# A pre-activation convolution on one core: contrasts in one small matmul, fewer columns, packed bias, fillers, and whole-image transfers

## The chip, the cores and the metric

The kernel runs on one core of a Trainium2 chip. The metric is the device time of one execution in microseconds. Three runs of the kernel before gave 89.01, 90.0 and 90.27 us; the median is 90.0.

## The reference

For each of 8 images with 32 channels of 128 x 128 the input is normalized over 16 groups (2 channels each), convolved with a 3 x 3 kernel of 32 output channels, given a bias, and added to the input. The convolution is written with Fourier transforms on 256 x 256, and what is cut out of it starts at (256 - 128) / 2:

```python
sh = (fft_H - out_h) // 2          # 64
out = sp[:, :, sh:sh + out_h, sw:sw + out_w]
return out + bias[None, :, None, None]
...
m = jnp.mean(g, axis=(2, 3, 4), keepdims=True)   # per group of 2 channels
s = jnp.var(g, axis=(2, 3, 4), keepdims=True)
return ((g - m) / jnp.sqrt(s + eps)).reshape(v.shape)
...
x = x + _L0_conv_ref(_gn(x), weight, bias, 1, 1)
```

So output pixel (0, 0) takes what an ordinary full convolution has at (64, 64). The lower right part of the image, 66 x 66 pixels with a border, is all that the convolution reads, and its result is non-zero only in the upper left 66 x 66 of the output. Everywhere else the output is the input plus the bias.

## The kernel before

**Layout.** The host splits every image into its four pixel parities. A core sees each image as a tile `x` of 128 partitions (2 row parities x 2 column parities x 32 channels) by 64 x 64 pixels, 2 MB in f32. All 8 images stay in SBUF. A 3 x 3 convolution becomes 2 x 2 taps of full 128 x 128 matrices in this layout. N is 33: a convolution reads pixels 31 to 63 in both directions, and writes rows and columns 0 to 32.

**Transfers.** SP issues every transfer but one, in program order: the first image in four pieces, the weights `w_sb`, then each image in two halves (line 68); later the stores of line 176. The bias, 128 rows of 4 bytes, is issued by ACT (line 71). SP's transfers take eight semaphores in turn, so each transfer waits on SP until the one eight issues earlier has landed. Transfers of one queue are worked off in the order of issue.

**Statistics.** For each image DVE runs eight `bn_stats` (line 109) and an aggregate (`mv`, line 116). PE multiplies the means with `avg`, which averages over the eight partitions of a group (`ps_m`, line 120); DVE takes three small steps (lines 125 to 128); PE averages the deviations and variances (`ps_v`, line 134). ACT takes the root (line 140), DVE the reciprocal and the product with the mean (lines 142, 143), and ACT writes the normalized pixels to `g` (line 147), a 34 x 34 tile whose last row and column are zeros; there are two of them, used in turn. ACT then adds the bias to the parts of the image that the convolution does not touch (lines 153 and 155).

**Convolution.** `multiply` covers 11 of the 33 rows in four matmuls of 363 columns, one for each tap (line 162); in f32 each shows as two records in the trace. `add` (line 171) adds the bias and the image to the sum, in place in `x`. A loop over the images writes the order out by hand: it puts the small matmuls of the next image between the chunks of the present one, and the statistics of the image after that between the `add`s. The lower half of an image (rows 33 to 63) is stored as soon as its bias is added, the upper part after its third `add`.

Of the kernel before, what the change touches and what calls it, by code (L numbers as in the profile page):

```python
# [24 lines left out]
F32 = mybir.dt.float32  # L25
AF = mybir.ActivationFunctionType
ALU = mybir.AluOpType

P = 128
EPS = 1e-5  # L30
FFT = 256
STATS = 8


@with_exitstack
def conv_preact_kernel(
    ctx: ExitStack,
    tc: tile.TileContext,
    x: bass.AP,
    weight: bass.AP,  # L40
    bias: bass.AP,
    out: bass.AP,
):
    nc = tc.nc

    B, _, H, W = x.shape
    C = P // 4
    LO = (FFT - 2 * H) // 4 - 1
    N = H - LO
    ROWS = 11  # L50
    NCHUNK = N // ROWS
    NSTAT = H // STATS

    cpool = ctx.enter_context(tc.tile_pool(name="const", bufs=1))
    xpool = ctx.enter_context(tc.tile_pool(name="x", bufs=1))
    spool = ctx.enter_context(tc.tile_pool(name="small", bufs=2))
    ps_conv = ctx.enter_context(tc.tile_pool(name="ps_conv", bufs=6, space=bass.MemoryType.PSUM))
    ps_stat = ctx.enter_context(tc.tile_pool(name="ps_stat", bufs=1, space=bass.MemoryType.PSUM))


    xts = [xpool.tile([P, H, W], F32, name=f"x{img}") for img in range(B)]
    w_sb = cpool.tile([P, 4, P], F32, name="w_sb")
    bias_sb = cpool.tile([P, 1], F32, name="bias_sb")
    for img in range(B):
        parts = 4 if img == 0 else 2
        for k in range(parts):
            rows = slice(k * H // parts, (k + 1) * H // parts)
            nc.sync.dma_start(xts[img][:, rows, :], x[img, :, rows, :])  # L68
        if img == 0:
            nc.sync.dma_start(w_sb, weight)  # L70
            nc.scalar.dma_start(bias_sb, bias)


    pair = cpool.tile([P, P // 2, 2], F32, name="pair")
    nc.gpsimd.memset(pair, 0.125)
    nc.gpsimd.affine_select(  # L76
        out=pair, in_=pair, pattern=[[-2, P // 2], [0, 2]], base=0,
        channel_multiplier=1, compare_op=ALU.is_ge, fill=0.0,
    )
    nc.gpsimd.affine_select(  # L80
        out=pair, in_=pair, pattern=[[2, P // 2], [0, 2]], base=1,
        channel_multiplier=-1, compare_op=ALU.is_ge, fill=0.0,
    )
    pair2 = pair.rearrange("p a b -> p (a b)")
    avg = cpool.tile([P, P], F32, name="avg")
    nc.vector.tensor_add(avg[:, 0 : 2 * C], pair2[:, 0 : 2 * C], pair2[:, 2 * C : 4 * C])  # L86
    nc.vector.tensor_add(avg[:, 2 * C : 3 * C], avg[:, 0:C], avg[:, C : 2 * C])
    for k in (0, 1, 3):
        nc.vector.tensor_copy(avg[:, k * C : (k + 1) * C], avg[:, 2 * C : 3 * C])
    eps = cpool.tile([P, 1], F32, name="eps")  # L90
    nc.vector.memset(eps, EPS * FFT * FFT)

    warm = cpool.tile([P, 1], F32, name="warm")
    nc.scalar.activation(warm, eps, AF.Sqrt)  # L94


    gs = []
    for k in range(2):
        g = cpool.tile([P, N + 1, N + 1], F32, name=f"g{k}")
        nc.gpsimd.memset(g[:, N : N + 1, :], 0.0)  # L100
        nc.gpsimd.memset(g[:, 0:N, N : N + 1], 0.0)
        gs.append(g)

    stats = [cpool.tile([P, NSTAT, 6], F32, name=f"stats{img}") for img in range(B)]
    mvs, ps_ms, ps_vs, means = {}, {}, {}, {}

    def take_stats(img, first, last):
        for s in range(first, last):
            nc.vector.bn_stats(  # L109
                stats[img][:, s, :],  # L110
                xts[img][:, STATS * s : STATS * (s + 1), :].rearrange("p h w -> p (h w)"),
            )

    def aggregate(img):
        mvs[img] = spool.tile([P, 2], F32, tag="mv", bufs=3, name=f"mv{img}")
        nc.vector.bn_aggr(mvs[img], stats[img].rearrange("p n s -> p (n s)"))  # L116

    def group_mean(img):
        ps_ms[img] = ps_stat.tile([P, 1], F32, tag="ps_m", name=f"ps_m{img}")
        nc.tensor.matmul(ps_ms[img], avg, mvs[img][:, 0:1], start=True, stop=True)  # L120

    def deviations(img):

        means[img] = spool.tile([P, 2], F32, tag="mean", name=f"mean{img}")
        nc.vector.tensor_copy(means[img][:, 0:1], ps_ms[img])  # L125
        diff = means[img][:, 1:2]
        nc.vector.tensor_sub(diff, mvs[img][:, 0:1], means[img][:, 0:1])  # L127
        nc.vector.scalar_tensor_tensor(  # L128
            diff, in0=diff, scalar=diff, in1=mvs[img][:, 1:2], op0=ALU.mult, op1=ALU.add
        )  # L130

    def group_variance(img):
        ps_vs[img] = ps_stat.tile([P, 1], F32, tag="ps_v", name=f"ps_v{img}")
        nc.tensor.matmul(ps_vs[img], avg, means[img][:, 1:2], start=True, stop=True)  # L134

    def normalize(img):
        xt, g = xts[img], gs[img % 2]

        std = spool.tile([P, 1], F32, tag="std", name=f"std{img}")
        nc.scalar.activation(std, ps_vs[img], AF.Sqrt, bias=eps, scale=float(FFT * FFT))  # L140
        rstd = spool.tile([P, 2], F32, tag="rstd", name=f"rstd{img}")
        nc.vector.reciprocal(rstd[:, 0:1], std)  # L142
        nc.vector.scalar_tensor_tensor(  # L143
            rstd[:, 1:2], in0=means[img][:, 0:1], scalar=-1.0, in1=rstd[:, 0:1],
            op0=ALU.mult, op1=ALU.mult,
        )
        nc.scalar.activation(  # L147
            g[:, 0:N, 0:N], xt[:, LO:H, LO:W], AF.Identity,
            bias=rstd[:, 1:2], scale=rstd[:, 0:1],
        )  # L150

        low = xt[:, N:H, :].rearrange("p h w -> p (h w)")
        nc.scalar.activation(low, low, AF.Identity, bias=bias_sb)  # L153
        right = xt[:, 0:N, N:W]
        nc.scalar.activation(right, right, AF.Identity, bias=bias_sb)  # L155

    def multiply(img, n):
        g = gs[img % 2]
        ps = ps_conv.tile([P, ROWS, N], F32, tag="ps", name=f"ps{img}_{n}")
        for k in range(4):  # L160
            top, left = n * ROWS + k // 2, k % 2
            nc.tensor.matmul(  # L162
                ps, w_sb[:, k, :], g[:, top : top + ROWS, left : left + N],
                start=(k == 0), stop=(k == 3),
            )
        return ps

    def add(img, n, ps):

        part = xts[img][:, n * ROWS : (n + 1) * ROWS, 0:N]  # L170
        nc.vector.scalar_tensor_tensor(  # L171
            part, in0=ps, scalar=bias_sb, in1=part, op0=ALU.add, op1=ALU.add
        )

    def store(img, first, last):
        nc.sync.dma_start(out[img, :, first:last, :], xts[img][:, first:last, :])

    take_stats(0, 0, NSTAT)
    aggregate(0)
    group_mean(0)  # L180
    deviations(0)
    group_variance(0)
    normalize(0)
    store(0, N, H)
    take_stats(1, 0, NSTAT)
    aggregate(1)
    for img in range(B):
        more, yet_more = img + 1 < B, img + 2 < B
        ps = multiply(img, 0)
        if more:  # L190
            group_mean(img + 1)
            deviations(img + 1)
        add(img, 0, ps)
        if yet_more:
            take_stats(img + 2, 0, NSTAT // 2)
        ps = multiply(img, 1)
        if more:
            group_variance(img + 1)
            normalize(img + 1)
            store(img + 1, N, H)  # L200
        add(img, 1, ps)
        if yet_more:
            take_stats(img + 2, NSTAT // 2, NSTAT)
            aggregate(img + 2)
        ps = multiply(img, 2)
        add(img, 2, ps)
        store(img, 0, N)


# [36 lines left out]
```

## Time and profile before

| | before |
|---|---|
| median of three runs | 90.0 us |
| the profiled execution | 90.13 us |
| its span | 88.2 us |
| PE busy | 67.2 us (76%) |
| DVE busy | 60.6 us (69%) |
| ACT busy | 37.9 us (43%) |
| moved by DMA | 33.84 MB, 384 GB/s over the span |

Busy times are summed over the span; the span is the time from the first to the last event of one profiled execution, and the execution's own time has 1.93 us beside it. The page divides the span into 40 slices of 2.2 us; a digit is a busy share in tenths. A window row gives a stretch's start and end, its length, the granted PE clock, the share in which the 16 DMA engines were busy (it can pass 1 in short stretches, since packets are counted where they start), and GB/s. A row of the chain or of the timeline gives start, length, engine, line and what ran.

### The profile page before, as it was taken

Reading aid. Unit: us, or ns where it says so; the run is one execution under the profiler, and the core shown is the slowest. Engines: PE = TensorE matmul, PEld = TensorE weight load, DVE = VectorE, ACT = ScalarE, POOL = GpSimd, SP = SyncE. Lnnn points to the kernel's source line nnn. Section 1 sums busy time; section 2 is a strip of 40 time slices with the busy share of each in tenths; the row PEclk is TensorE's granted clock in tenths of the full one; section 3 lists DMA queues with packets and bytes.
Section 4 is the critical chain, followed back from the end, with each engine's and each line's share of the span. In section 5 each row is a group of like instructions: output and inputs, shape, how many; then the busy total and the mean of one; then the engine's idle time right before and its main releaser. Section 6 shows DMA issues by size and latency. Waiting matters only on the chain.

```text
span 88.2 us, 744 instructions
## 1 busy us (share of the span) xinstructions
PE 67.2 (76%) x224; PEld 41.5 (47%) x224; DVE 60.6 (69%) x142; ACT 37.9 (43%) x34; POOL 2.1 (2%) x11
## 2 busy tenths in 40 slices
PE   0000022599999999999999999999999999999300
PEld 0000022356665665666566556656664666666000
DVE  0308965992999799979979997998899723222200
ACT  4200003970049517922980594189139707910000
POOL 6200000000000000000000000000000000000000
PEclk9999999999999999999999999999999999999997
DMA  1679999999999999999999999999999999799392
GB/s 20 160 283 420 441 416 416 424 416 416 416 424 428 428 420 413 424 416 424 405 415 436 428 422 420 422 439 428 423 427 419 437 431 426 306 401 424 153 391 100
DMA packets 5186, 33.84 MB, mean 384 GB/s; under 512 B 704, under 2 KB 704, under 8 KB 2368
## 3 DMA queue, kind: packets, MB, share of 16 engines
q1 hardware_dynamic: 5040, 33.82, 93.1%
q10 hardware_dynamic: 144, 0.00, 0.1%
q8 instruction: 1, 0.02, 0.1%
q14 instruction: 1, 0.01, 0.0%
HBM read 17.04 MB, written 16.78 MB: 384 GB/s over the span
## 4 chain that ended last, share of the span: by engine, by line
PE 76%; DMA 8%; DVE 7%; ACT 2%; issue 1%; SPq 0%; DVEq 0%
PE ps L162 73%; DMA x<-x_dram 8%; DVE stats L109 4%; PE ps_m L120 2%; PE ps_v L134 2%; ACT g L147 1%; DVE x L171 1%; DVE mv L116 0%; SPq L68 0%; ACT std L140 0%; DVE mean L128 0%; DVE rstd L142 0%; DVE rstd L143 0%; DVE mean L127 0%; DVE mean L125 0%
## 5 line engine op out<-in xcount | busy, mean ns | idle before, releaser
L162 PE MATMUL ps<-g,w_sb 128*128 128x363 f32 x192 | 65.9, 493 | 2.1 <-ACT g L147 2.1
L162 PEld LDWEIGHTS ps<-g,w_sb 128*128 128x128 f32 x192 | 36.1, 197 | 23.5 <-ACT g L147 5.2
L109 DVE BATCH_NORM_STATS2 stats<-x 128x6 f32<-128x512 f32 x64 | 39.5, 679 | 3.4 <-DMA x<-x_dram 3.4
L171 DVE SCALAR_TENSOR_TENSOR x<-ps,bias_sb,x 128x363 f32<-128x363 f32 x24 | 13.8, 576 | 7.0 <-PE ps L162 7.0
L153 ACT ACTIVATE x<-x,bias_sb 128x1984 f32<-128x1984 f32 x8 | 15.6, 1949 | 0.3
L140 ACT ACTIVATE std<-ps_v,eps 128x1 f32<-128x1 f32 x8 | 2.1, 261 | 31.4 <-PE ps_v L134 31.4
L147 ACT ACTIVATE g<-x,rstd 128x1089 f32<-128x1089 f32 x8 | 10.4, 1305 | 5.8 <-DVE rstd L143 4.9
L120 PE MATMUL ps_m<-mv,avg 128*128 128x1 f32 x16 | 2.7, 236 | 12.4 <-DVE mv L116 12.4
L120 PEld LDWEIGHTS ps_m<-mv,avg 128*128 128x128 f32 x16 | 3.4, 222 | 14.4 <-DVE mv L116 12.4
L155 ACT ACTIVATE x<-x,bias_sb 128x1023 f32<-128x1023 f32 x8 | 9.1, 1132 | 0.0
L125 DVE COPY mean<-ps_m 128x1 f32<-128x1 f32 x8 | 1.3, 158 | 5.5 <-PE ps_m L120 5.5
L134 PEld LDWEIGHTS ps_v<-mean,avg 128*128 128x128 f32 x16 | 3.1, 204 | 2.4 <-DVE mean L128 0.8
L116 DVE BATCH_NORM_AGGREGATE mv<-stats 128x2 f32<-128x48 f32 x8 | 3.0, 372 | 0.3
L142 DVE RECIPROCAL rstd<-std 128x1 f32<-128x1 f32 x8 | 1.2, 150 | 2.8 <-ACT std L140 2.8
L134 PE MATMUL ps_v<-mean,avg 128*128 128x1 f32 x16 | 2.5, 227 | 0.7 <-DVE mean L128 0.7
L86 DVE TENSOR_TENSOR avg<-pair 128x64 f32<-128x64 f32 x1 | 0.2, 226 | 2.6 <-POOL pair L80 2.6
L128 DVE SCALAR_TENSOR_TENSOR mean<-mean,mv 128x1 f32<-128x1 f32 x8 | 1.8, 220 | 0.3
L94 ACT ACT_TABLE_LOAD x1 | 1.3, 1283 | 1.2 <-PEq L234 1.2
L127 DVE TENSOR_TENSOR mean<-mv,mean 128x1 f32<-128x1 f32 x8 | 1.3, 159 | 0.3
L143 DVE SCALAR_TENSOR_TENSOR rstd<-mean,rstd 128x1 f32<-128x1 f32 x8 | 1.3, 160 | 0.3
L76 POOL TENSOR_SCALAR_AFFINE_SELECT pair<-pair 128x128 f32<-128x128 f32 x1 | 0.7, 706 | 0.1
L80 POOL TENSOR_SCALAR_AFFINE_SELECT pair<-pair 128x128 f32<-128x128 f32 x1 | 0.7, 706 | 0.1
(11 smaller groups left out, 1.9 us busy)
## 6 DMA issues: line engine op xcount, KB each, us to landing
x<-x_dram SPq DMA_DIRECT2D x14, 1024.0 KB, 19.0
out_dram<-x SPq DMA_DIRECT2D x8, 1056.0 KB, 14.2
out_dram<-x SPq DMA_DIRECT2D x8, 992.0 KB, 15.2
x<-x_dram SPq DMA_DIRECT2D x4, 512.0 KB, 7.3
w_sb<-weight_dram SPq DMA_DIRECT2D x1, 256.0 KB, 8.6
bias_sb<-bias_dram ACTq DMA_DIRECT2D x1, 0.5 KB, 6.0
```

The costliest lines, as they stand in the source:

```text
L94: nc.scalar.activation(warm, eps, AF.Sqrt)
L109: nc.vector.bn_stats(stats[img][:, s, :], xts[img][:, STATS * s : STATS * (s + 1), :].rearrange("p h w -> p (h w)"),)
L116: nc.vector.bn_aggr(mvs[img], stats[img].rearrange("p n s -> p (n s)"))
L120: nc.tensor.matmul(ps_ms[img], avg, mvs[img][:, 0:1], start=True, stop=True)
L128: nc.vector.scalar_tensor_tensor(diff, in0=diff, scalar=diff, in1=mvs[img][:, 1:2], op0=ALU.mult, op1=ALU.add)
L134: nc.tensor.matmul(ps_vs[img], avg, means[img][:, 1:2], start=True, stop=True)
L140: nc.scalar.activation(std, ps_vs[img], AF.Sqrt, bias=eps, scale=float(FFT * FFT))
L147: nc.scalar.activation(g[:, 0:N, 0:N], xt[:, LO:H, LO:W], AF.Identity, bias=rstd[:, 1:2], scale=rstd[:, 0:1],)
L153: nc.scalar.activation(low, low, AF.Identity, bias=bias_sb)
L155: nc.scalar.activation(right, right, AF.Identity, bias=bias_sb)
L162: nc.tensor.matmul(ps, w_sb[:, k, :], g[:, top : top + ROWS, left : left + N], start=(k == 0), stop=(k == 3),)
L171: nc.vector.scalar_tensor_tensor(part, in0=ps, scalar=bias_sb, in1=part, op0=ALU.add, op1=ALU.add)
```

## The change

- **Transfers.** The first image is loaded in pieces of 8, 16, 16, 16 and 8 rows, the second in pieces of 32, 16 and 16, all others whole. Images 0 to 5 are stored whole after the last `add`; images 6 and 7 in parts. The bias and a small matrix `signs` lie behind the weights in one tile `wb_sb`, which SP loads; ACT issues no transfer.
- **Statistics.** ACT multiplies `signs` by each partition's mean and scales the variance (`terms`, 9 columns). One small matmul with `avg` gives minus the group mean, seven contrasts of the eight means of a group, and the mean variance. ACT squares the contrasts and sums them; with the mean variance this is the group variance. DVE copies one column and takes the reciprocal.
- **Convolution.** `g` is 33 x 33 and has no zeros; taps that would read them leave that row or column out. `g` is written in two parts, the first 12 rows first.
- **Fillers.** Five matmuls with 512 columns on pieces of the first image stand ahead of its small matmul, three behind it. Their results are not read.
- **Order.** The third `add` of an image stands behind the next image's aggregate; two chunks are multiplied before the small matmul, one after.

```diff
-    w_sb = cpool.tile([P, 4, P], F32, name="w_sb")
-    bias_sb = cpool.tile([P, 1], F32, name="bias_sb")
+    wb_sb = cpool.tile([P, 4 * P + 1 + NSIGN], F32, name="wb_sb")
+    bias_sb = wb_sb[:, 4 * P : 4 * P + 1]
+    signs = wb_sb[:, 4 * P + 1 :]
     for img in range(B):
-        parts = 4 if img == 0 else 2
-        for k in range(parts):
-            rows = slice(k * H // parts, (k + 1) * H // parts)
+        pieces = {0: (1, 2, 2, 2, 1), 1: (4, 2, 2)}.get(img, (8,))
+        first = 0
+        for piece in pieces:
+            rows = slice(first, first + piece * STATS)
             nc.sync.dma_start(xts[img][:, rows, :], x[img, :, rows, :])
+            first += piece * STATS
         if img == 0:
-            nc.sync.dma_start(w_sb, weight)
-            nc.scalar.dma_start(bias_sb, bias)
+            nc.sync.dma_start(wb_sb, wb)
...
+        terms = spool.tile([P, NSIGN + 1], F32, tag="terms", name=f"terms{img}")
+        nc.scalar.activation(terms[:, 0:NSIGN], signs, AF.Identity, scale=mv[:, 0:1])
+        nc.scalar.activation(
+            terms[:, NSIGN:], mv[:, 1:2], AF.Identity, bias=eps, scale=float(FFT * FFT)
         )
...
+        nc.tensor.matmul(ps_ms[img], avg, mvs[img], start=True, stop=True)
...
+        nc.scalar.activation(square, contrasts, AF.Square, accum_out=var[:, 0:1])
+        nc.vector.tensor_copy(var[:, 1:2], ps_m[:, NSIGN:])
...
+        nc.scalar.activation(std, var[:, 0:1], AF.Sqrt, bias=var[:, 1:2])
...
+        nc.scalar.activation(rstd[:, 1:2], ps_m[:, 0:1], AF.Identity, scale=rstd[:, 0:1])
+        for rows in (slice(0, ROWS + 1), slice(ROWS + 1, N)):
...
+            dr, dc = k // 2, k % 2
+            rows = min(ROWS, N - dr - n * ROWS)
+            top = n * ROWS + dr
             nc.tensor.matmul(
-                ps, w_sb[:, k, :], g[:, top : top + ROWS, left : left + N],
+                ps[:, 0:rows, 0 : N - dc], wb_sb[:, k * P : (k + 1) * P],
+                g[:, top : top + rows, dc:N],
...
+    for first, times in ((0, 1), (1, 1), (3, 1), (5, 1), (7, 1)):
+        keep_warm(first * STATS, times)
     take_stats(0, 0, NSTAT)
     aggregate(0)
-    group_mean(0)
-    deviations(0)
-    group_variance(0)
+    group(0)
+    keep_warm(0, 3)
     normalize(0)
-    store(0, N, H)
+    add_bias(0)
     take_stats(1, 0, NSTAT)
-    aggregate(1)
     for img in range(B):
-        more, yet_more = img + 1 < B, img + 2 < B
-        ps = multiply(img, 0)
+        more = img + 1 < B
+        ps = [multiply(img, 0), multiply(img, 1)]
         if more:
-            group_mean(img + 1)
-            deviations(img + 1)
-        add(img, 0, ps)
-        if yet_more:
-            take_stats(img + 2, 0, NSTAT // 2)
-        ps = multiply(img, 1)
+            aggregate(img + 1)
+        if img:
+            add(img - 1, 2, last)
+            if img - 1 < B - 2:
+                store(img - 1, 0, H)
+            else:
+                for k in range(B - 2, B):
+                    store(k, N, H)
+                store(img - 1, 0, N)
+        add(img, 0, ps[0])
         if more:
-            group_variance(img + 1)
+            group(img + 1)
             normalize(img + 1)
...
+            add_bias(img + 1)
+        add(img, 1, ps[1])
+        last = multiply(img, 2)
+        if img + 2 < B:
+            take_stats(img + 2, 0, NSTAT)
+    store(B - 1, 0, 2 * ROWS)
+    add(B - 1, 2, last)
+    store(B - 1, 2 * ROWS, N)
```

What now stands where, in rows of the order of each engine (line, operation, written tile <- read tiles, shape; `x_72` to `x_79` are the eight images).

ACT at the program's start, of the kernel before and then of the change:

```order
L71 DMA bias_sb<-bias_dram 128x1
L94 ACT_TABLE_LOAD
L94 ACTIVATE warm<-eps 128x1
L140 ACTIVATE std_148<-ps_v_146,eps 128x1
L147 ACTIVATE g_116<-x_72,rstd_150 128x33x33
L153 ACTIVATE x_72<-x_72,bias_sb 128x1984
```

```order
L96 ACT_TABLE_LOAD
L96 ACTIVATE warm<-eps 128x1
L114 ACTIVATE terms_136<-wb_sb,mv_134 128x8
L115 ACTIVATE terms_136<-mv_134,eps 128x1
L131 ACTIVATE square_144,var_145<-ps_m_139 128x7
L135 ACTIVATE std_148<-var_145 128x1
L138 ACTIVATE rstd_150<-ps_m_139,rstd_150 128x1
L140 ACTIVATE g_110<-x_72,rstd_150 128x396
```

The bias transfer is gone from ACT's queue, and five small operations stand in an image's chain ahead of `g` where one stood.

SP behind its loads, from the first store on, of the kernel before and then of the change:

```order
L176 DMA out_dram<-x_72 128x1984
L176 DMA out_dram<-x_73 128x1984
L176 DMA out_dram<-x_72 128x2112
L176 DMA out_dram<-x_74 128x1984
L176 DMA out_dram<-x_73 128x2112
L176 DMA out_dram<-x_75 128x1984
```

```order
L176 DMA out_dram<-x_72 128x4096
L176 DMA out_dram<-x_73 128x4096
L176 DMA out_dram<-x_74 128x4096
L176 DMA out_dram<-x_75 128x4096
L176 DMA out_dram<-x_76 128x4096
L176 DMA out_dram<-x_77 128x4096
L176 DMA out_dram<-x_78 128x1984
L176 DMA out_dram<-x_79 128x1984
L176 DMA out_dram<-x_78 128x2112
L176 DMA out_dram<-x_79 128x1408
L176 DMA out_dram<-x_79 128x704
```

The lower half of an image no longer goes ahead of the image before it; it waits for the upper part.

DVE for one image in the loop, of the kernel before (from the first `add` of image 1) and then of the change (from the third `add` of image 0):

```order
L171 SCALAR_TENSOR_TENSOR x_73<-ps_0_213,bias_sb,x_73 128x11x33
L109 BN_STATS stats_125<-x_75 128x6 x4
L142 RECIPROCAL rstd_238<-std_236 128x1
L143 SCALAR_TENSOR_TENSOR rstd_238<-mean_220,rstd_238 128x1
L171 SCALAR_TENSOR_TENSOR x_73<-ps_1_229,bias_sb,x_73 128x11x33
L109 BN_STATS stats_125<-x_75 128x6 x4
L116 BN_AGGR mv_250<-stats_125 128x2
L171 SCALAR_TENSOR_TENSOR x_73<-ps_2_252,bias_sb,x_73 128x11x33
```

```order
L171 SCALAR_TENSOR_TENSOR x_72<-ps_2_197,wb_sb,x_72 128x11x33
L171 SCALAR_TENSOR_TENSOR x_73<-ps_0_210,wb_sb,x_73 128x11x33
L132 COPY var_231<-ps_m_228 128x1
L137 RECIPROCAL rstd_236<-std_234 128x1
L171 SCALAR_TENSOR_TENSOR x_73<-ps_1_215,wb_sb,x_73 128x11x33
L104 BN_STATS stats_115<-x_75 128x6 x8
L112 BN_AGGR mv_267<-stats_115 128x2
```

The eight `bn_stats` now stand in one piece behind the reciprocal, with the aggregate behind them, and no other work of DVE lies between.

More of the change, by code (lines that the diff above doesn't have):

```diff
@@ L39, in conv_preact_kernel @@
     x: bass.AP,
-    weight: bass.AP,
-    bias: bass.AP,
+    wb: bass.AP,
     out: bass.AP,
@@ L83, in conv_preact_kernel @@
     )
+    eps = cpool.tile([P, 1], F32, name="eps")
+    nc.vector.memset(eps, EPS * FFT * FFT)
     pair2 = pair.rearrange("p a b -> p (a b)")
@@ L89, in conv_preact_kernel @@
         nc.vector.tensor_copy(avg[:, k * C : (k + 1) * C], avg[:, 2 * C : 3 * C])
-    eps = cpool.tile([P, 1], F32, name="eps")
-    nc.vector.memset(eps, EPS * FFT * FFT)
     warm = cpool.tile([P, 1], F32, name="warm")
     nc.scalar.activation(warm, eps, AF.Sqrt)
[L97 to L102, printed above, removed]
+    gs = [cpool.tile([P, N, N], F32, name=f"g{k}") for k in range(2)]
     stats = [cpool.tile([P, NSTAT, 6], F32, name=f"stats{img}") for img in range(B)]
-    mvs, ps_ms, ps_vs, means = {}, {}, {}, {}
+    mvs, ps_ms = {}, {}
     def take_stats(img, first, last):
@@ L114, in aggregate @@
     def aggregate(img):
[L115 to L129, printed above, removed]
-        )
@@ L132, in group_variance @@
-    def group_variance(img):
-        ps_vs[img] = ps_stat.tile([P, 1], F32, tag="ps_v", name=f"ps_v{img}")
-        nc.tensor.matmul(ps_vs[img], avg, means[img][:, 1:2], start=True, stop=True)
+        mv = spool.tile([P, 2], F32, tag="mv", name=f"mv{img}")
+        nc.vector.bn_aggr(mv, stats[img].rearrange("p n s -> p (n s)"))
+        terms = spool.tile([P, NSIGN + 1], F32, tag="terms", name=f"terms{img}")
+        nc.scalar.activation(terms[:, 0:NSIGN], signs, AF.Identity, scale=mv[:, 0:1])
@@ L139, in normalize @@
         std = spool.tile([P, 1], F32, tag="std", name=f"std{img}")
-        nc.scalar.activation(std, ps_vs[img], AF.Sqrt, bias=eps, scale=float(FFT * FFT))
+        nc.scalar.activation(std, var[:, 0:1], AF.Sqrt, bias=var[:, 1:2])
         rstd = spool.tile([P, 2], F32, tag="rstd", name=f"rstd{img}")
         nc.vector.reciprocal(rstd[:, 0:1], std)
[L143 to L150, printed above, removed]
+        nc.scalar.activation(rstd[:, 1:2], ps_m[:, 0:1], AF.Identity, scale=rstd[:, 0:1])
+        for rows in (slice(0, ROWS + 1), slice(ROWS + 1, N)):
+            nc.scalar.activation(
+                g[:, rows, :], xt[:, LO + rows.start : LO + rows.stop, LO:W], AF.Identity,
+                bias=rstd[:, 1:2], scale=rstd[:, 0:1],
+            )
@@ L160, in multiply @@
         for k in range(4):
-            top, left = n * ROWS + k // 2, k % 2
+            dr, dc = k // 2, k % 2
+            rows = min(ROWS, N - dr - n * ROWS)
+            top = n * ROWS + dr
             nc.tensor.matmul(
-                ps, w_sb[:, k, :], g[:, top : top + ROWS, left : left + N],
+                ps[:, 0:rows, 0 : N - dc], wb_sb[:, k * P : (k + 1) * P],
+                g[:, top : top + rows, dc:N],
                 start=(k == 0), stop=(k == 3),
@@ L176, in store, with keep_warm @@
         nc.sync.dma_start(out[img, :, first:last, :], xts[img][:, first:last, :])
+    ps_w = ps_stat.tile([P, 512], F32, tag="ps_w", name="ps_w")
+    def keep_warm(first, times):
+        piece = xts[0][:, first : first + STATS, :].rearrange("p h w -> p (h w)")
+        for _ in range(times):
+            nc.tensor.matmul(ps_w, avg, piece, start=True, stop=True)
+    for first, times in ((0, 1), (1, 1), (3, 1), (5, 1), (7, 1)):
+        keep_warm(first * STATS, times)
     take_stats(0, 0, NSTAT)
     aggregate(0)
-    group_mean(0)
-    deviations(0)
-    group_variance(0)
+    group(0)
+    keep_warm(0, 3)
     normalize(0)
-    store(0, N, H)
+    add_bias(0)
     take_stats(1, 0, NSTAT)
-    aggregate(1)
     for img in range(B):
-        more, yet_more = img + 1 < B, img + 2 < B
-        ps = multiply(img, 0)
+        more = img + 1 < B
+        ps = [multiply(img, 0), multiply(img, 1)]
         if more:
-            group_mean(img + 1)
-            deviations(img + 1)
-        add(img, 0, ps)
-        if yet_more:
-            take_stats(img + 2, 0, NSTAT // 2)
-        ps = multiply(img, 1)
+            aggregate(img + 1)
[8 more added lines that the diff above has]
+        add(img, 0, ps[0])
         if more:
-            group_variance(img + 1)
+            group(img + 1)
             normalize(img + 1)
[L200 to L207, printed above, removed]
+            add_bias(img + 1)
[6 more added lines that the diff above has]
+    store(B - 1, 2 * ROWS, N)
 def kernel(x, L0_conv_weight, L0_conv_bias):
@@ L225 @@
                 blocks[rin, cin, :, dr, dc, rout, cout, :] = weight[:, :, a, b].T
+    bits = [(-1.0) ** (np.arange(4 * C) // k % 2) for k in (2 * C, C, 1)]
+    signs = -np.ones((4 * C, NSIGN), x.dtype)
+    for k in range(1, NSIGN):
+        signs[:, k] = FFT * np.prod([b for j, b in enumerate(bits) if k >> j & 1], axis=0)
     arrays = {
@@ L230 @@
         ).reshape(B, 4 * C, H // 2, W // 2),
-        "weight_dram": blocks.reshape(4 * C, 4, 4 * C),
-        "bias_dram": np.tile(np.asarray(L0_conv_bias).reshape(C, 1), (4, 1)),
+        "wb_dram": np.concatenate(
+            [
+                blocks.reshape(4 * C, 16 * C),
+                np.tile(np.asarray(L0_conv_bias).reshape(C, 1), (4, 1)),
+                signs,
+            ],
+            axis=1,
+        ),
     }
```

11 lines of the change are left out of this document (10 added, 1 removed).

## The prediction

> **What bounds the kernel now.** The first view is the page's chain of the work that ended last, and beside it the slices and the DMA queue.
>
> ```profile
> span 88.2 us, 744 instructions
> PE 76%; DMA 8%; DVE 7%; ACT 2%; issue 1%; SPq 0%; DVEq 0%
> DMA  1679999999999999999999999999999999799392
> GB/s 20 160 283 420 441 416 416 424 416 416 416 424 428 428 420 413 424 416 424 405 415 436 428 422 420 422 439 428 423 427 419 437 431 426 306 401 424 153 391 100
> q1 hardware_dynamic: 5040, 33.82, 93.1%
> ```
>
> The chain puts 76% of the span on PE, which says: shorten the matmuls. The DMA rows say something else. One queue (q1, issued by SP) carries 33.82 MB and keeps 16 engines busy for 93.1% of the span. Both can hold at once: PE runs without a gap from 16 us on and the last store waits for it, but a queue that is full from the fourth slice to the thirty-fourth will not end sooner because PE does. So the second view is the same traffic in stretches; its last two columns are the DMA engines' busy share and GB/s.
>
> ```profile
> 6.60:9.20 2.60, 1.00 1.03 419
> 10.00:20.00 10.00, 1.00 1.02 423
> 20.00:30.00 10.00, 1.00 1.01 420
> 62.00:75.00 13.00, 1.00 1.01 426
> ```
>
> Loads (10 to 30 us) run at 420 to 423 GB/s, stores (62 to 75) at 426, at a share of 1. No long stretch is faster. 33.82 MB at 425 GB/s is 79.6 us of an 88.2 us span. The 8.6 us that remain are the start, two holes at the end, and the fixed ends. What the change is worth is read there, unless compute becomes so slow that stores come late.
>
> **The start.** Third view: the same columns for the first microseconds, then the queues in the stretch 2.6:5.2, the issue row of the bias, and SP's issues of loads (start, us, count).
>
> ```profile
> 1.80:2.60 0.80, 1.00 0.69 133
> 2.60:5.20 2.60, 1.00 0.66 166
> 5.20:6.00 0.80, 1.00 0.79 302
> 6.00:6.60 0.60, 1.00 0.99 403
> q1 hardware_dynamic: 114, 0.43, 64.0%
> q10 hardware_dynamic: 110, 0.00, 2.1%
> bias_sb<-bias_dram ACTq DMA_DIRECT2D x1, 0.5 KB, 6.0
> 0.80 1.88 SPq L68 DMA_DIRECT2D x<-x_dram  x4
> 3.56 23.07 SPq L68 DMA_DIRECT2D x<-x_dram  x14
> ```
>
> Four 512 KB loads were issued by 2.7 us, yet for 2.6 us the engines move 166 GB/s at a share of 0.66. In that stretch there are 114 packets of q1 and 110 of q10, one to one. q10 is the bias transfer on ACT's queue: 144 packets for half a kilobyte, 6.0 us from issue to landing. Where q10 runs out, the rate goes to 302 and 403. The change packs the bias behind the weights, so q10 goes. If it holds the engines up, the stretch gains 2.6 x (1 - 166/419) = 1.57 us and the next 0.8 x (1 - 302/419) = 0.22, **1.8 us** at most. If the slowness is only that of a first transfer, it gains **0**: the stretch 1.8 to 2.6, where q10 has no packets yet, has 133 GB/s as well. I take **1.5**, because the one-to-one count, the idle third of the engines and the time of the recovery all point at q10.
>
> The Trainium skill speaks on both sides here. "DMA: Bandwidth & Descriptors", section "Queues, rings and completion order", has each DMA engine take turns between queues packet by packet; the counts 114 and 110 agree, and by it the term is near 1.8. The same page, section "Issuing engines are not separate DMA queues", says that transfers of several issuers simply interleave and that a second issuer saves only issue time; by it half a kilobyte costs nothing and the term is 0.
>
> **The end.** Same columns, then SP's issues in that stretch, and the landings of all stores (shortest, median, longest).
>
> ```profile
> 76.00:76.40 0.40, 1.00 0.86 359
> 76.40:76.80 0.40, 1.00 0.35 148
> 76.80:77.20 0.40, 1.00 0.25 106
> 77.20:77.60 0.40, 1.00 0.81 341
> 82.00:83.00 1.00, 1.00 0.39 161
> 83.00:84.00 1.00, 1.00 0.12 51
> 86.40:88.20 1.80, 0.67 0.00 0
> 76.54 6.94 SPq L176 DMA_DIRECT2D out_dram<-x  x3
> DMA to landing us min/median/max: 3.9/14.7/20.8
> ```
>
> The last three stores are issued between 76.54 and 83.5 (the last at 83.15, since one issue takes 0.33). The engines stand idle for 0.4 x (0.14 + 0.65 + 0.75 + 0.19) = 0.69 us in the first hole and 0.61 + 0.88 = 1.49 in the second: **2.2 us** in the mean. The last store lands at 83.15 + 3.9 = 87.05, and the span ends 1.1 later. But the mean isn't the slowest engine. In the bottom of the first hole a share of 0.25 is left: four engines of sixteen still work on old stores while the others have nothing. They lose nothing there, and in the second hole only what follows their own last packet; new data starts near 83.9, and a share of 0.39 in 82 to 83 says that some worked to about 83.2. A queue that never runs dry ends with these engines, so it recovers some **0.7 us** (bounds 0.5 and 2.2).
>
> **Packet size.** Loads become 128x4096 and six stores 128x4096, where 128x2048, 1984 and 2112 stood. From 4 KB rows (419 GB/s, 6.6 to 9.2) to 8 KB rows (420 to 423) the rate rose by about 0.6%; another doubling may give half of it, 0.3% of some 70 us: **0.2 us** (bounds 0, and 0.5 at the full 0.6%).
>
> **The compute side, and why I cost it at nothing.** Rows of the chain in order of time, of the timeline and of the page.
>
> ```profile
> 16.38 5.21 PE ps L162 x8
> 21.81 2.79 PE ps L162 x8
> 72.50 9.89 PE ps L162 x32
> 12.01 0.38 DVE mv L116
> 12.43 0.60 PE ps_m L120 x2
> 15.03 1.31 ACT g L147
> 14.91 4.84 DVE L109 BATCH_NORM_STATS2 stats<-x 128x6 f32<-128x512 f32 x8
> 62.39 0.59 DVE L171 SCALAR_TENSOR_TENSOR x<-ps,bias_sb,x 128x363 f32<-128x363 f32 x1
> 62.90 2.46 DVE L109 BATCH_NORM_STATS2 stats<-x 128x6 f32<-128x512 f32 x4
> L140 ACT ACTIVATE std<-ps_v,eps 128x1 f32<-128x1 f32 x8 | 2.1, 261 | 31.4 <-PE ps_v L134 31.4
> L116 DVE BATCH_NORM_AGGREGATE mv<-stats 128x2 f32<-128x48 f32 x8 | 3.0, 372 | 0.3
> L142 DVE RECIPROCAL rstd<-std 128x1 f32<-128x1 f32 x8 | 1.2, 150 | 2.8 <-ACT std L140 2.8
> L94 ACT ACT_TABLE_LOAD x1 | 1.3, 1283 | 1.2 <-PEq L234 1.2
> ```
>
> The fillers: the first eight records take 5.21 us, the next eight 2.79, so a warm PE saves about 2.4. The first chain, from the aggregate at 12.01 to the convolution at 16.38, also shrinks: one small matmul pair (0.60) goes with three small DVE operations (about 0.6), the first 12 rows of `g` take about 0.6 of the 1.31, and two ACT terms come (0.5): some 3.0 in place of 4.4. With data 1.5 earlier the convolution starts at 13.5, or 15 if the eight fillers hold it up. Per image: 9.89/32 = 0.309 us a record; 4225 columns in place of 4356 give 24 x 0.309 x 0.97 = 7.2, and with one small pair 7.4. None of this is in the sum, because the queue below covers it.
>
> DVE's order has a longer loop. Behind the small matmul: square (0.26), copy (0.16), root (0.26), reciprocal (0.15), with hops 0.95; one `add` (0.51 to its successor); eight `bn_stats` 4.84; the aggregate 0.4; two ACT terms 0.55; the matmul, between 0.28 warm and 0.60 cold, 0.45. Together **7.7 us per image** (it was 8.01). The square with a summed output and the two terms have no row. The nearest ACT rows are 0.26 on one column (L140) and 1.31 on 1089 (`g`); with seven, eight and one columns I take 0.26 each. At the other end three of them would add 3 x 1.05 = 3.2 to the loop: the price of the slower rival below. The waiting `copy` holds up only the reciprocal, the next `add` and the next image's statistics behind it on DVE, which are in this sum.
>
> The first small matmul inside the loop stands behind two chunks (4.8): near 19. The whole store of image k follows small matmul k+1, at 19 + 7.7 k, by 0.95 + 0.51 + 4.84 + 0.4 + 0.5 = 7.2; image 5 is issued at 64.7. The queue ends the 17.04 MB of loads near 2.6 + 17.0/0.421 = 43, then takes 2.10/0.426 = 4.93 per image and reaches image 5 at 67.6. So it does not starve, by 2.9 us. PE ends near 19 + 6 x 7.7 + 2.4 + 7.2 = 74.8 (the last chunk of image 6, then image 7), some 6 us before the queue reaches the last pieces. The whole-image store, which waits for rows that were sent earlier before, is thus hidden by the backlog; without that cover it costs what it comes late. SP waits before each DMA for the one eight issues earlier; with longer transfers the loads are all issued by about 12 us, not 26.6, and each store's predecessor has landed long before.
>
> **Sum.** 1.5 + 0.7 + 0.2 = 2.4. Span 88.2 - 2.4 = 85.8. The profiled execution took 90.13 (1.93 beyond its span; the median of three is 90.0): 90.13 - 2.4 = **87.7 us**. Counting forward agrees: 67.6 + 4.93 + 4.19/0.426 is 82.4 for the mean engine, about 2 more for the last, and landing with the fixed end 1.4.
>
> **Rivals.**
> - *The ramp is not the bias's* (0.25): nothing gained at the start. 0.7 + 0.2 = 0.9, so 89.2 us. For it: 133 GB/s before q10's first packet. This is where the second rule of the Trainium skill leads, in the section on issuing engines.
> - *All idle time is recovered* (0.09): 1.8 + 2.2 + 0.5 = 4.5, so 85.6. Against it: the four late engines.
> - *PE was the bound after all* (0.02): 74.8, an add 0.6, a last store of 0.36 MB in 3.9 - 0.72/0.426 = 2.2, end 1.1: span 78.7, 80.6 us. It needs over 450 GB/s throughout.
> - *Stores come a little late* (0.06): a loop of 8.4 to 9.3 us lets the queue run dry in places, 88.3 to 90.
> - *Slower: the loop outlasts the queue* (0.06). Square and root alternate on ACT; two table loads of 1.28 per image (or a square as slow as bounded above, three times over) would make the loop 10.3: 19 + 61.8 + 9.6 + 0.6 + 2.2 + 1.1 = 94.3, 96.2 us. It loses time from a loop of 9.3 on. Against it: the built order has one table load.
>
> **How the numbers follow.** The forecast has 0.52, with a range of its own from 86.7 to 88.5. A measurement of this kernel can tell about 2% from no change: faster means below 88.2. The forecast gives 0.44 of its 0.52 to that, full recovery 0.09, PE 0.02, the first rival 0.01: 0.56. Within 2%: 0.08 + 0.24 + 0.06 = 0.38. Slower: 0.06. The range goes from 86.4 to 89.5: it holds the forecast, the first rival and most late stores, and leaves out 0.09 + 0.02 + 0.06 and a little of the rest.
>
> **What would show it.** No q10; 2.6 to 5.2 above 350 GB/s; DMA share near 1 from about 4 us to the end with no hole; PE finished about 9 us before the last landing, so the chain ends in DMA; a PE period near 7.7; eight first records near 2.6 us. Wrong if the stretch to 5.2 stays near 170 (then 89.2), if the queue has holes after 45 us, or if a rate well off 425 appears with 16 KB rows: 1% of it is 0.8 us.

## The result

The changed kernel took 87.34 us (median of four runs, 87.06 to 89.21) against 89.85 before (four runs): a ratio of 0.972, 95% interval 0.964 to 0.980. The forecast was 87.7 us. In a second comparison on another chip, beside 17 runs of the kernel before, it had 87.48 against 89.57, 0.978 (0.974 to 0.983). The ratios and ranges of spans here and below leave out runs in a slower state, more than 1.5% above the fastest of their kernel, such as the 89.21.

The page of the changed kernel, first the parts that answer to those shown of before: the span, the chain's share by engine, the DMA slices, and the queues.

```profile
span 85.8 us, 764 instructions
DMA  1999989999999999999999999999999999999950
GB/s 34 267 372 416 436 300 460 428 435 428 443 412 443 435 416 443 405 435 420 443 405 447 420 435 420 443 420 443 428 435 428 435 428 406 419 422 428 408 235 11
q1 hardware_dynamic: 3744, 33.82, 94.5%
PE 82%; DMA 4%; DVE 1%; issue 1%; DVEq 0%
```

The span is 2.4 us shorter. The queue's row is full from the second slice to the thirty-eighth, but for an 8 in the sixth, and the two holes near the end are gone; q10 does not appear. The chain still names PE, now with 82%. Read how far it goes: its shares add up to 88%. The chain is followed back from the last *instruction*; the 10.5 us behind it, in which the queue empties, are in no share.

The chain in order of time, first and last pieces (start, length, what):

```profile
14.30 4.81 PE ps L161 x16
19.23 7.21 PE ps L161 x24
26.48 0.39 PE ps_m L123 x2
65.04 9.53 PE ps L161 x32
74.66 0.60 DVE x L171
```

The convolution starts warm at 14.3 (16.38 before, and cold), an image takes 7.21 + 0.42 = 7.63 us, and the last `add` begins at 74.66, 7.8 us earlier than before. Of these 7.8 us the span kept 2.4. Where these come from is seen in the traffic, in windows of the same columns as before: start and end, length, granted clock, DMA share, GB/s. The kernel before, then the changed one:

```profile
0.00:6.60 6.60, 1.00 0.53 155
6.60:75.00 68.40, 1.00 1.01 423
```

```profile
0.00:6.60 6.60, 1.00 0.68 230
2.60:5.20 2.60, 1.00 0.89 303
6.60:75.00 68.40, 1.00 1.01 425
82.00:83.00 1.00, 0.50 0.62 248
83.00:84.00 1.00, 0.50 0.20 79
84.00:85.00 1.00, 0.50 0.03 11
```

By 6.6 us the changed kernel has moved 1.52 MB in place of 1.02: 0.5 MB at 423 GB/s are **1.2 us**. From there to 75 us it moves 2 GB/s more, 0.14 MB or **0.3 us**. The rest of the 2.4, some **0.9 us**, is put down to the end, as what is left over and not as a measurement of its own: there is no hole, and the queue runs out while shares of 0.62, 0.20 and 0.03 show the late engines alone. These three rows hold 0.38 + 0.80 + 0.97 = 2.15 us of idle time in the mean, about as much as the two holes had. So the idle time has moved from the holes to the end of the queue.

### The profile page after: what moved, and what is told of

It is laid out like the page before. It is cut to its first block, busy times and chain, and to the rows that moved or that the text cites. A ratio compares the mean times of both kernels' runs of the same rounds, so it can differ in the third digit from the quotient of the medians.

```text
span 85.8 us, 764 instructions
## 1 busy us (share of the span) xinstructions
PE 70.0 (82%) x224; PEld 40.9 (48%) x224; DVE 56.8 (66%) x118; ACT 48.5 (57%) x82; POOL 1.8 (2%) x7
## 4 chain that ended last, share of the span: by engine, by line
PE 82%; DMA 4%; DVE 1%; issue 1%; DVEq 0%
PE ps L161 67%; PE ps_w L184 11%; DMA x<-x_dram 4%; PE ps_m L123 3%; DVE x L171 1%; DVEq L171 0%
## 5 line engine op out<-in xcount | busy, mean ns | idle before, releaser
L161 PE MATMUL ps<-g,wb_sb 128*128 128x363 f32 (+1 forms) x192 | 58.7, 462 | 0.0
L161 PEld LDWEIGHTS ps<-g,wb_sb 128*128 128x128 f32 x192 | 35.3, 189 | 19.9 <-ACT g L140 1.9
L171 DVE SCALAR_TENSOR_TENSOR x<-ps,wb_sb,x 128x363 f32<-128x363 f32 x24 | 13.2, 569 | 6.3 <-PE ps L161 6.3
L149 ACT ACTIVATE x<-x,wb_sb 128x1984 f32<-128x1984 f32 x8 | 15.6, 1949 | 0.3
L184 PE MATMUL ps_w<-x,avg 128*128 128x512 f32 x16 | 9.9, 778 | 4.3 <-DMA x<-x_dram 4.3
L140 ACT ACTIVATE g<-x,rstd 128x396 f32<-128x396 f32 (+1 forms) x16 | 12.7, 839 | 0.3
L151 ACT ACTIVATE x<-x,wb_sb 128x1023 f32<-128x1023 f32 x8 | 9.1, 1133 | 0.0
L184 PEld LDWEIGHTS ps_w<-x,avg 128*128 128x128 f32 x16 | 3.7, 245 | 8.9 <-DVE avg L93 4.3
L123 PEld LDWEIGHTS ps_m<-terms,avg 128*128 128x128 f32 x16 | 2.5, 188 | 4.4 <-ACT terms L115 4.2
L123 PE MATMUL ps_m<-terms,avg 128*128 128x9 f32 x16 | 3.0, 260 | 0.2
```

Of the source, the lines that this page charges most:

```text
L123: nc.tensor.matmul(ps_ms[img], avg, mvs[img], start=True, stop=True)
L140: nc.scalar.activation(g[:, rows, :], xt[:, LO + rows.start : LO + rows.stop, LO:W], AF.Identity, bias=rstd[:, 1:2], scale=rstd[:, 0:1],)
L161: nc.tensor.matmul(ps[:, 0:rows, 0 : N - dc], wb_sb[:, k * P : (k + 1) * P], g[:, top : top + rows, dc:N], start=(k == 0), stop=(k == 3),)
L171: nc.vector.scalar_tensor_tensor(part, in0=ps, scalar=bias_sb, in1=part, op0=ALU.add, op1=ALU.add)
L184: nc.tensor.matmul(ps_w, avg, piece, start=True, stop=True)
```

## The experiments

Ratios below are to the kernel before, run beside each kernel on the same chip.

### The bias alone, and the bias put back

The kernel before, with the bias behind the weights (`wb_sb` has 4 * P + 1 columns; the shapes are left out here):

```diff
-            nc.sync.dma_start(w_sb, weight)
-            nc.scalar.dma_start(bias_sb, bias)
+            nc.sync.dma_start(wb_sb, wb)
```

> The kernel before with one edit: the bias lies behind the weights and is loaded with them by SP, so ACT issues no transfer. Theory (the bias transfer's packets hold up the engines at the start): the stretch 2.6 to 5.2 us goes from 166 GB/s to 300 or more, the first image is complete about 1.6 us earlier, and the whole execution is 1.2 to 1.6 us shorter: 88.3 to 88.7 us against 89.85. Rival (the slow start is that of any first transfer): 166 GB/s stays, and the time stays within 0.3 us of 89.85.

Measured: 88.26 us, 0.989 (0.985 to 0.994). The window and the queue of 2.6 to 5.2 us:

```profile
2.60:5.20 2.60, 1.00 0.91 293
q1 hardware_dynamic: 203, 0.76, 90.6%
```

293 GB/s where there were 166, and 1.0 us gained of the 1.2 to 1.6 expected. So in the kernel before, the bias transfer does cost about a microsecond. The changed kernel with the bias back on ACT's queue, read out of the packed rows:

```diff
+            nc.scalar.dma_start(bias_sb, wb[:, 4 * P : 4 * P + 1])
```

> The changed kernel with one edit: the bias is loaded again as 128 rows of 4 bytes on ACT's queue. Theory: the stretch 2.6 to 5.2 us falls from 303 GB/s to about 170, and the time grows by 1.2 us, to 88.5. Rival: no difference, 87.3.

```profile
2.60:5.20 2.60, 1.00 0.88 319
q1 hardware_dynamic: 262, 0.83, 85.7%
q10 hardware_dynamic: 105, 0.00, 2.2%
```

This is a miss of the mechanism: 105 packets of the bias stand beside the loads, and the stretch has 319 GB/s and not the 170 expected; the span is 85.3 us. The time, 88.25, did come out near the 88.5 expected, but not in the span: its six runs have 2.4 to 3.2 us outside the span, where most other runs have 1.7 to 2.0. That was not explained. So a second queue alone cannot be the whole cause. Two differences to the kernel before were left: where the bias is read from, and the size of the first loads. To have the two kernels on one chip, both were run again unchanged.

> The kernel before, unchanged, for a second profile. If the bias's queue or anything else of the program slows the start, 2.6 to 5.2 us shows about 166 GB/s again; if the slow start was a matter of that one execution, it shows about 300.

> The changed kernel, unchanged, on the chip of the runs beside it: 0.972 of before, and 300 GB/s in 2.6 to 5.2 us.

```profile
2.60:5.20 2.60, 1.00 0.67 153
q1 hardware_dynamic: 106, 0.40, 64.9%
q10 hardware_dynamic: 108, 0.00, 2.0%
```

These are of the kernel before: 153 GB/s, the slow start again. The changed kernel showed 311 GB/s and a span of 85.1. With the bias as a tensor of its own, as before the change:

```diff
+            nc.scalar.dma_start(bias_sb, bias)
...
+        "bias_dram": np.tile(np.asarray(L0_conv_bias).reshape(C, 1), (4, 1)),
```

> The changed kernel with the bias loaded by ACT from a tensor of its own, 128 values of 4 bytes side by side, as before the change; with the bias read out of the packed tensor's rows (2084 bytes apart) the start stayed fast at 319 GB/s beside 105 packets of the bias. Theory A (all engines read one half kilobyte of memory at once and wait for each other): 2.6 to 5.2 us falls to about 170 GB/s and the span grows by about 1.2 us. Theory B (one-to-one turns of two queues cost nothing, and the slow start came from the order or size of the first loads): 300 GB/s or more, span as in the changed kernel.

```profile
2.60:5.20 2.60, 1.00 0.86 274
q10 hardware_dynamic: 93, 0.00, 1.9%
```

274 GB/s, a little under the 300 of theory B, but span 85.2 and ratio 0.978 (0.974 to 0.983), as the changed kernel beside it. Theory A falls. The size of the first loads remained, and was tried on both sides. In the changed kernel with that bias tensor, the first image in four pieces of 16 rows again:

```diff
-        pieces = {0: (1, 2, 2, 2, 1), 1: (4, 2, 2)}.get(img, (8,))
+        pieces = {0: (2, 2, 2, 2), 1: (4, 2, 2)}.get(img, (8,))
```

> The changed kernel with the bias on ACT from its own tensor, and the first image in four pieces of 16 rows as before the change (first pieces have rows of 4 KB, not 2 KB). Theory (on each engine eight packets of the bias take turns one to one with the first eight of the loads, and a turn costs more with 4 KB): 2.6 to 5.2 us falls to about 160 GB/s and the span grows by about 1 us against the changed kernel. Rival (something else of the program before slowed its start): 270 GB/s or more.

And in the kernel before, the other way round:

```diff
-        parts = 4 if img == 0 else 2
+        for piece in (1, 2, 2, 2, 1) if img == 0 else (4, 4):
...
```

> The kernel before with one edit: the first image in pieces of 8, 16, 16, 16 and 8 rows; the bias stays on ACT's queue. Theory: with 2 KB rows in the first piece the turns with the bias are over sooner, 2.6 to 5.2 us rises from 155 GB/s to about 270, and 0.7 to 1.0 us is gained. Rival: 155 GB/s and no gain.

The changed kernel first, then the kernel before:

```profile
2.60:5.20 2.60, 1.00 0.68 161
q1 hardware_dynamic: 109, 0.42, 66.5%
q10 hardware_dynamic: 108, 0.00, 2.0%
```

```profile
2.60:5.20 2.60, 1.00 0.81 260
q10 hardware_dynamic: 95, 0.00, 1.8%
```

Both rates are as expected. With 4 KB rows first, the changed kernel falls to 161 GB/s; its span is 86.1 us, 0.6 more than the median of the runs with the same bias and 2 KB rows first, on another chip, and not the 1 expected; its ratio of 0.983 (0.978 to 0.989) overlaps with their 0.978. With 2 KB rows first, the kernel before rises to 260 GB/s and gains 0.9 us: 88.75 against 89.62, 0.990 (0.985 to 0.995). So the slow start takes two things together: the bias on a second queue *and* a first piece of 16 rows. Either edit of the change brings 0.9 to 1.0 us in the kernel before; of the two together no more than that was seen.

Shorter stretches show how the row size enters. The same two runs, in the same order:

```profile
2.20:3.80 1.60, 1.00 0.63 159
3.80:5.40 1.60, 1.00 0.68 162
```

```profile
2.20:3.80 1.60, 1.00 0.67 163
3.80:5.40 1.60, 1.00 0.97 357
```

Rows of 2 KB do not escape the slow rate; it ends sooner. While the bias has packets, the two queues' packets stand nearly one to one: 93 and 92 from 3 to 5 us with 4 KB rows, 118 and 120 from 2.2 to 3.8 us with 2 KB rows. On 16 engines that is a turn of both queues in 0.34 us and in 0.22 us (0.34 to 0.46 in the four profiles with the bias and 4 KB rows first, 0.19 to 0.22 in the three with the bias and 2 KB). The 144 packets of the bias are nine for each engine in the mean, and they last until about 6 us in the one case and about 4 us in the other. Why a turn takes so long, where 4 KB at 423 GB/s take an engine 0.155 us, these runs do not settle.

### The fillers and PE

> The changed kernel without its eight filler matmuls. Theory (the queue sets the end): the first eight records of the convolution take 5.2 us again in place of about 2.4, PE ends 2 to 3 us later, near 77, still before the queue's last store; time unchanged within 0.3 us of 87.3. Rival (PE sets the end, as the chain of waits says): 2.4 us more, 89.7.

```profile
13.67 8.12 PE ps L161 x16
77.34 0.60 DVE x L171
```

Without fillers the first sixteen records take 8.12 us in place of 4.81 and the last `add` begins at 77.34 in place of 74.66. The time stays: 0.979 (0.975 to 0.984), with the changed kernel at 0.978. The fillers, 2.7 us of PE, are worth nothing here that these runs can tell. Without them the cover is nearly used up, though: image 5's store is issued at 67.27, and the share falls to 0.58 from 67.2 to 67.6 us and to 0.20 from 67.6 to 68.0. In the kernel before they were added alone (their result takes one of the six buffers of `ps`, so five are left):

> The kernel before with the eight fillers alone: PE is warm when the convolution starts, and ends about 2.1 us earlier. Theory (the queue sets the end): the holes before the last stores close, and 0.7 us is gained. Rival (PE sets the end): all 2.1 us are gained.

```profile
14.85 4.77 DVE stats L109 x8
20.07 0.38 PE ps_m L120 x2
81.13 0.60 DVE x L171
```

88.82 us against 89.57, 0.993 (0.990 to 0.996): the 0.7 us expected. But this kernel does not tell the two theories apart, since PE did not end earlier than in the second profile of the kernel before (81.12 for the last `add`): warm, PE finishes its first chunk and then waits for the statistics of image 1, which DVE ends at 19.6, so the small matmul stands at 20.07. What it brought may be less variation, which is argued and not shown. In the second profile of the kernel before, the first records took less than in the first, where they had 5.21:

```profile
16.18 4.16 PE ps L162 x8
81.12 0.60 DVE x L171
81.00:82.00 1.00, 1.00 0.43 177
82.00:83.00 1.00, 1.00 0.56 237
82.20:82.40 0.20, 1.00 0.10 42
```

The last `add` was 1.4 us earlier, the span 87.1 in place of 88.2, and of the two holes one is left, with 0.57 + 0.44 = 1.0 us of idle time in the mean where the two had 2.2. At its bottom the share is 0.10, one or two engines of sixteen. So in that execution there was less to lose. With fillers the spans lie between 86.6 and 87.6, against 86.7 to 88.1 without.

How much PE time the queue covers was tried from the other side.

```diff
+    fill = cpool.tile([P, 512], F32, name="fill")
+    nc.gpsimd.memset(fill, 0.5)
...
         ps = [multiply(img, 0), multiply(img, 1)]
+        for _ in range(1):
+            nc.tensor.matmul(ps_w, avg, fill, start=True, stop=True)
```

> The changed kernel with one more 512-column matmul per image in the loop, ahead of the small matmul (0.86 us of PE each, 6.9 in all; its result is not read). The loop becomes 8.5 us, PE ends near 81.3, and image 5's store is issued near 69.7, when the early engines have waited up to 2 us and the late ones not at all. Theory (the queue sets the end, and covers up to about 9.3 us a loop): at most 0.5 us more than the changed kernel. Rival (PE sets the end): 6.9 us more.

```profile
66.00:67.00 1.00, 1.00 0.84 360
67.00:68.00 1.00, 1.00 0.66 279
68.00:69.00 1.00, 1.00 0.39 164
79.63 0.60 DVE x L171
```

88.86 us, 0.991 (0.988 to 0.995): some 1.3% over the changed kernel's 0.978, 1.1 us. The last `add` begins 5.0 us later, since the loop became 8.19 us and not 8.5. So some four fifths of the added PE time disappear under the queue, but not all: between 66 and 69 the engines stand idle for 0.16 + 0.34 + 0.61 = 1.1 us, while SP waits for image 5's last `add` and issues its store at 68.14. (By the spans, 86.9 to 87.3 against 85.0 to 85.5, the loss is larger, about 1.7.) At most 0.5 was expected, so this is a miss: the cover ends at a loop of about 8, earlier than I had it.

### The row size

> The changed kernel with images 2 to 7 loaded and images 0 to 5 stored in two halves, issued one behind the other at the same places: rows of 8 KB where 16 KB stood, nothing else. By the rates seen (loads 429 against 420 GB/s, stores 434 against 427) the packet size is worth about 0.85 us: 88.2. By the term of the prediction, 0.2: 87.5. If size does nothing: 87.3.

```diff
-        pieces = {0: (1, 2, 2, 2, 1), 1: (4, 2, 2)}.get(img, (8,))
+        pieces = {0: (1, 2, 2, 2, 1), 1: (4, 2, 2)}.get(img, (4, 4))
...
-                store(img - 1, 0, H)
+                store(img - 1, 0, H // 2)
+                store(img - 1, H // 2, H)
```

Loads, then stores, of the changed kernel (16 KB rows), and then of this one (8 KB):

```profile
20.00:30.00 10.00, 1.00 1.00 429
50.00:62.00 12.00, 1.00 1.02 434
```

```profile
20.00:30.00 10.00, 1.00 1.01 424
50.00:62.00 12.00, 1.00 1.01 427
```

Ratio 0.986 (0.982 to 0.990), where the kernel without fillers beside it, equal to the changed one in time, had 0.979: without the larger rows 0.6 us are lost. The spans show it too, 86.0 to 86.8 with the halves and 85.1 to 86.0 without. The rates fall back to those before the change or close to them. The size of a row and that of a transfer changed together here, so the loss is not shown to be the row's alone.

### A try at a faster version

```diff
-        pieces = {0: (1, 2, 2, 2, 1), 1: (4, 2, 2)}.get(img, (8,))
+        pieces = {0: (1, 2, 2, 2, 1), 1: (4, 4)}.get(img, (8,))
...
+    def store_15(img, first, last):
+        for p in (slice(0, 120), slice(120, P)):
+            nc.sync.dma_start(out[img, p, first:last, :], xts[img][p, first:last, :])
...
```

> A try at a faster version: the changed kernel without fillers, with the second image loaded in two halves (its 16-row pieces ran at about 340 GB/s between 11 and 13 us in place of 420), and with the last two stores split into partitions 0 to 119 and 120 to 127, so that one engine has no part in the large ones. The halves should give 420 GB/s between 11 and 13 us and 0.3 us. If the engine left out is one of those that end 1.5 to 2 us late, the end comes up to 1 us sooner; if it is another, 0.1 to 0.2 us later.

```profile
11.00:13.00 2.00, 1.00 1.00 422
80.00:81.00 1.00, 1.00 0.92 293
82.00:83.00 1.00, 0.50 0.84 284
83.00:84.00 1.00, 0.50 0.90 242
```

88.24 us, 0.981 (0.975 to 0.988): no gain. There were 422 GB/s between 11 and 13 us; but the two kernels with the bias tensor, which kept the 16-row pieces of the second image, had 397 and 410 there, so the pieces alone do not make that stretch slow. In this profile the end got worse: the last stores ran at 240 to 290 GB/s at shares of 0.8 to 0.9, so the transfers of the split were slow in themselves. The queue also had a hole at 67 to 68 us (share 0.43), as without fillers above. The profiled execution, 88.89 us, is one of the two longest of six, and the other four took 87.42 to 88.28, so what held these back is not shown. Whether the engine left out was a late one was not seen. No version tried beats the changed kernel.

## Why the prediction was right, and where not

**The bound was right.** The queue sets the end: 7.8 us less on the way to the last `add` came with a span only 2.4 us shorter, giving back the fillers' 2.7 us changed nothing that the runs can tell, and adding 5.0 us of PE cost 1.1. The reading that decided it was the share of 1 in long windows beside a chain that named PE.

**The size was right, partly by cancelling.** Predicted 2.4, measured 2.4 in the profiled execution, and 2.5 and 2.1 by the medians of the two comparisons. Some of the match is luck: the forecast starts from a span of 88.2, at the upper end of the kernel's executions (86.7 to 88.1 in the second comparison), and the terms, whose sum comes out because the end is what is left over, missed to both sides:
- *The start*, 1.5 (bounds 0 and 1.8): 1.2 in the trace, 1.0 from the packed bias alone. I expected 350 GB/s or more in 2.6 to 5.2; it was 303, and 311, 336, 346, 372 and 374 in the five other profiles that begin with 2 KB rows and no second queue. In these six, the stretch from 2.2 to 3.8 us has 204 to 330 GB/s, so a start without any second queue is slow for a while too. And I gave the term to one edit. The one-to-one packet counts did point at the right queue, but they alone decide nothing: while the bias lasts they stand with 2 KB rows first too (118 to 120), where little is lost. The rule of the Trainium skill on turns between queues ("DMA: Bandwidth & Descriptors", "Queues, rings and completion order") fits the packets while both queues have some, 93 to 92 and 118 to 120; what it costs depended on the first loads. The other rule of the Trainium skill, on a second issuer ("Issuing engines are not separate DMA queues" on the same page), held for the time of the changed kernel, 0.978 with and without a bias on ACT's queue, and failed for the one before, where the bias cost 1.0 us.
- *The end*, 0.7 (0.5 to 2.2): about 0.9 is left over for it. The reasoning by the late engines fits: the mean idle time of 2.2 was not recovered, it stands behind 82 us. But the term belongs to that execution. In the second profile of the kernel before, PE was warm sooner and 1.0 us of idle time stood in the hole, so in the median it is probably worth less.
- *Row size*, 0.2 (0 to 0.5): **this term was mis-sized.** The halves cost 0.6 us, outside the bound. I halved the step from 4 to 8 KB of a short window; from 8 to 16 KB the rates rose from 420 to 429 and from 427 to 434. In the profiled execution the stretch from 6.6 to 75 us gained only 0.3. The loads of image 1 ran slow between 11 and 13 us (the slice with 300 GB/s), 295 GB/s against 406 before, which is 0.5 us.

**The compute side was right in nearly all its numbers**, though it was in no term: start of the convolution 13.5 to 15 (14.3), loop 7.7 (7.63), last `add` after 74.8 (74.66). That the loop came out is partly luck. I had 7.7 from DVE's order and 7.4 for PE; in the trace PE sets it, busy for 9.97 of the 10 us from 20 to 30 where DVE has 9.16. PE's matmuls of an image took the 7.2 forecast; the small pair and the gap took 0.42 and not 0.2. The square is two instructions, 178 and 194 ns, where I had 0.26; it did not show.

**Two details were wrong.** The chain does not end in DMA; it cannot show what comes after the last instruction. And the cover: I let the loop go to 9.3 us before time is lost in earnest, and 8.19 already cost 1.1. My own figures had it nearer: 2.9 us between image 5's store and the queue, spread over five loops, are used up at a loop of 8.3.

**The rivals.** That the start is not the bias's is refuted for the kernel before. Full recovery and PE as the bound did not occur, no store came late in the changed kernel, since the queue's row has no hole, and the square brought no table load (one in the whole program): the slower rival had no ground.

## What to carry to other kernels

Before pricing an engine's work, put the bytes over the rate of the longest full window beside the span: here 79.6 of 88.2 us were spoken for, and only the start and the end of the queue could give anything. Follow a queue's end by its latest engine, not by the mean, and look whether the profiled execution is a typical one before taking a hole at its end for a term. When two edits touch the same moment, test each alone and both away: two that remove the same loss don't add.

## What the hardware showed that I had not expected

A half-kilobyte transfer of 144 packets on a second queue cost about 1 us at the start (0.989), and nothing that the time shows when the loads beside it began with 2 KB rows (0.978 with it and without). Loads with rows of 16 KB ran at 423 to 436 GB/s from 20 to 30 us in eight profiles, with rows of 8 KB at 419 to 424 in six; stores from 50 to 62 us at 429 to 434 and 426 to 428: about 2% and 1%. And a queue that the page calls one of instructions takes time of the engines too: its packet took 4.8% of 16 engines' time in 1.4 us, which is one engine for 1.07 us.

```profile
q8 instruction: 1, 0.02, 4.8%
```

It lies in 34.0 to 35.4 us of the changed kernel. Whether such packets make the late engines late was not tried.
